# The written order of a graph layer's steps: a step's sums are turned back two shares and the queries' projection later, and a tile is joined behind that

## The chip, the core and the metric

The kernel runs on one core of a Trainium2 chip. The metric is the time of one launch on the device in microseconds, the median of seven runs. One further execution was taken with the hardware profiler; all durations below come from it.

## The reference, cut to what matters

Two layers work on 3125 nodes with 256 numbers each and on 100000 edges. A layer adds three things to its input: a graph attention over the edges, a token mixer, and then a feed-forward part. Only layer 0's graph attention and mixer bear on the change:

```
xn = layernorm(x)
x  = x + gnn(xn, edges) + mix(xn)           # layer 0; mix: 4 blocks of linear attention + GELU MLP
# gnn: two convolutions, each followed by batch norm and leaky relu
q, k, v = x @ wq, x @ wk, x @ wv            # 4 heads of 64
alpha   = sum(q[dst] * k[src], head) / 8
a       = softmax of alpha over the edges of one dst
out     = segment_sum(a * v[src], dst) + x @ ws
```

`gnn` and `mix` read the same input and do not need each other, so that the kernel can run them side by side.

## The kernel before, in words

Layer 0 puts the nodes in order of their number of edges and cuts them into 25 tiles of 128 nodes. Each tile has as many slots for edges as its largest node needs (64 in the first tile, 22 in the last, 833 in all). A tile's slots are worked off in two to four **steps** of one or two sub-steps with at most eight slots each; a convolution has 63 steps, the two convolutions 126. The rows of keys and values for one slot (512 numbers a node) are fetched by one indirect DMA that GpSimd issues (L707). Four buffers `kv` hold a sub-step each, so that the rows of step n+1 are fetched while step n is worked on; a buffer is free again when TensorE has read its values.

What a step does is written as letters, and the string `PATTERN` gives their order. Each letter issues instructions on the engines that it names, and TensorE, VectorE and ScalarE execute them exactly in that order, one engine by itself, waiting for each other by semaphores. GpSimd and SyncE are ordered by the scheduler. Read for step n:

- `K1`, `K0`: VectorE multiplies keys by queries and sums per head, for the second sub-step of n and the first of n+1 (L1074, L1077).
- `S`, `E`: VectorE takes bias and maximum (L1087 to L1091), ScalarE the exponential (L1101).
- `V0`, `V1`: VectorE sums the weights (L1108) and multiplies the values by them (L1114).
- `P0`, `P1b`: TensorE sums the values over the slots by transposing matmuls that accumulate (L200); `P1b` is that of step n-1's second sub-step. What comes out in PSUM is transposed.
- `Rb`, `Xb`, `Yb`: the sums of step n-1 are brought back. ScalarE copies them to SBUF (`accT`, L1133), TensorE turns them by two transposes into the other half of their PSUM tile (L214), ScalarE copies that to `res` (L1141).
- `M`, `N`: in a tile's last step, the maxima and sums of its steps are brought together (L1149 to L1167).
- `J`, `O`, `U`: in a tile's first step, the tile before is finished. `J` (VectorE, L1175) weighs the parts in `res` with each other, `O` (TensorE, L1555 and L1562) turns them and adds the skip projection, `U` adds the bias on ScalarE (L1570), takes the batch norm's statistics on VectorE (L1575) and stores.
- `T`, `B`: in the same step the next tile's nodes are turned (L1524) and brought to SBUF. `Q`: in a tile's second step its successor's queries are projected (L1538 and the bias at L129).
- `m`: one share of the mixer. The mixer is a list of small pieces, each with a part on TensorE and a `post` on ScalarE or VectorE that evicts it; five `m` stand in a step, and each takes as many pieces as are due. A piece's post is issued one piece after its TensorE part.

The mixer's lines in what follows: L189 projections, L1682 turned rows, L1751 keys, L1792, L1806, L1835 and L1960 attention, L1991 and L2009 the MLP with its bias at L129, L2017 and L1968 the additions to the result on VectorE.

The sums and the tile's output take their PSUM from one pool, `cps`, with two buffers; the queries from another with two; the mixer's pieces from a third with four. A step's sums keep their `cps` buffer from `P0` until `Yb` of the next step. Layer 1 has a pattern of its own, which is not touched.

These lines tie the letters to the functions:

```
P0=(True, lambda: self.sums(n, 0)),
P1b=(was["two"], lambda: self.sums(n - 1, 1)),
Rb=(n > 0, lambda: self.result(n - 1)),
Xb=(n > 0, lambda: self.turned(n - 1)),
Yb=(n > 0, lambda: self.kept(n - 1)),
J=(first and i > 0, lambda: self.join(i - 1)),
O=(first and i > 0, lambda: self.tiles[i - 1]["out"][0]()),
Q=(c == 1, lambda: self.q.__setitem__(i + 1, make())),
m=(True, lambda: mix(3 / PATTERN.count("m"))),
```

Of the kernel before, what the change touches and what calls it, by code (L numbers as in the profile page):

```python
# [1016 lines left out]
    sent.append(ins)  # L1017


PATTERN = "K1 m S E M P1b Rb m Xb Yb Q V0 J m P0 O V1 N m K0 T m U B".split()  # L1020


class SlotOrder:
# [156 lines left out]
    def run(self):  # L1180
# [18 lines left out]
        for n, t in enumerate(self.steps):  # L1199
# [8 lines left out]
            if more:  # L1208
# [25 lines left out]
                Q=(c == 1, lambda: self.q.__setitem__(i + 1, make())),  # L1234
                m=(True, lambda: mix(3 / PATTERN.count("m"))),
            )
            for what in PATTERN:
                if do[what][0]:
# [5 lines left out]
        for what, f in last.items():  # L1244
            if what in PATTERN and (what not in ("V1b", "P1b") or t["two"]):
                if what in ("Rb", "Xb", "Yb"):
                    f(n)
                else:
                    f(n, int(what[1]))
        if "Nb" in PATTERN:  # L1250
            self.join_sum(NQ - 1)
# [5 lines left out]
class EdgeOrder(SlotOrder):  # L1257


    HEADS, SCALE = 8, 1.0 / math.sqrt(32.0)  # L1260
    PATTERN = (
        "P1b D2 Rb D3 m K1 T0 Xb Yb S E M J m E0 Qt Qb m T1 D0 O m U Qm E1 Qk V0 m D1 T2 m "
        "V1 E2 m P0 T3 N m E3 K0 m"
    ).split()
# [86 lines left out]
    def run(self, ended):  # L1351
# [10 lines left out]
        self.keys(0, 0)  # L1362
        parts = self.PATTERN.count("m")
        for n, t in enumerate(self.steps):
# [2433 lines left out]
```

## Time and profile before

| | |
|---|---|
| median of 7 runs | 5315.23 us (5305.73 to 5320.78) |
| the profiled execution, its own time | 5315.53 us |
| its span in the profile | 5313.7 us |
| mean granted TensorE clock | 0.851 |
| busy: TensorE, VectorE, ScalarE, GpSimd | 4062, 3909, 1714, 3080 us |
| steps of convolution 1 | from 331 to 1490 us |
| steps of convolution 2 | from 1594 to 2787 us |

The profiled execution is 0.3 us above the median of the seven, so that sums made on it can be read as sums on the median. The change lies in the two stretches of steps, 2352 us together; everything else stays as it is. "Idle" of an engine is the time between the end of one of its instructions and the start of the next, and each idle stretch is put down to what ended last before it was over.

### The profile page before, as it was taken

To read this page: it belongs to the slowest core of one execution; us is meant where nothing else is said; L and a number is where in the kernel's file an instruction comes from. 1 tells how busy PE (TensorE), PEld (TensorE's weight loads), DVE (VectorE), ACT (ScalarE), POOL (GpSimd) and SP (SyncE) were. 2 spreads that over 40 slices of the span, in tenths; PEclk is the share of its full clock that TensorE was granted. 3 is DMA by queue.
4 is the path that set the end of the run, shared out by engine and by line. 5 is a ranking of instruction groups with operands and counts; after the bars stand their busy time and mean duration, and the time that the engine had idled before them with its cause. 6 is when DMAs were issued, how large, how long until landed. Compare 5 with 4: busy or idle time off the path is not lost. (4 is left out here: it accounts for less than half of the span.)

```text
span 5313.7 us, 54974 instructions
## 1 busy us (share of the span) xinstructions
PE 4062.2 (76%) x19016; PEld 2691.6 (51%) x19016; DVE 3909.2 (74%) x5861; ACT 1714.3 (32%) x3630; POOL 3080.3 (58%) x2945
## 2 busy tenths in 40 slices
PE   2557898768885688877885596987888887788778
PEld 1235675456644466555664463345455554444445
DVE  5268888878848888898873213469888888888957
ACT  1023334323342334443343111333333333333221
POOL 2466776657727577666753503257766767776720
PEclk8778999879997799988996797888788888888889
DMA  5166776667737577666765343545655655565610
GB/s 167 48 192 198 211 215 206 184 187 213 214 126 209 183 215 210 204 204 189 223 192 186 114 148 110 172 123 170 181 174 172 190 159 170 167 183 168 184 56 25
DMA packets 374305, 908.90 MB, mean 171 GB/s; under 512 B 94268, under 2 KB 170074, under 8 KB 373892
## 3 DMA queue, kind: packets, MB, share of 16 engines
q0 software_dynamic: 232624, 725.48, 46.3%
q1 hardware_dynamic: 134232, 165.02, 9.6%
q10 hardware_dynamic: 7162, 14.80, 0.7%
q8 instruction: 153, 2.51, 0.2%
q14 instruction: 134, 1.10, 0.1%
HBM read 813.62 MB, written 91.30 MB: 170 GB/s over the span
## 5 line engine op out<-in xcount | busy, mean ns | idle before, releaser
L707 POOL DMA_INDIRECT kv<-kvtab,slots x2499 | 2580.7, 1033 | 1144.0 <-issue 666.2
L1077 DVE TENSOR_REDUCE al<-kv 128x28 f32<-128x1792 f32 (+5 forms) x345 | 719.2, 2085 | 11.9
L200 PEld LDWEIGHTS cps<-ident,kv 128*128 128x128 f32 x4998 | 621.7, 152 | 145.7 <-issue 84.8
L200 PE MATMUL cps<-ident,kv 128*128 128x128 f32 x4998 | 670.7, 291 | 15.7 <-DVE kv L1114 10.4
L1316 DVE TENSOR_TENSOR kv<-kv,e 128x1024 f32<-128x1024 f32 x460 | 489.1, 1113 | 153.8 <-PE e L1305 63.4
L1074 DVE TENSOR_TENSOR kv<-kv,qa 128x1792 f32<-128x1792 f32 (+2 forms) x230 | 478.6, 2081 | 121.6 <-DMA kv<-kvtab,slots 100.6
L1114 DVE TENSOR_TENSOR kv<-kv,qa 128x1792 f32<-128x1792 f32 (+2 forms) x230 | 475.2, 2075 | 0.0
L1991 PE MATMUL mm<-hTm,w 128*128 128x500 f32 (+1 forms) x896 | 377.6, 563 | 28.8 <-DVE xcur L2017 23.6
L2009 PE MATMUL mm<-w,hid 128*125 128x256 f32 x1600 | 386.3, 391 | 11.0 <-ACT hid L1999 10.8
L2009 PEld LDWEIGHTS mm<-w,hid 128*125 128x125 f32 x1600 | 298.6, 195 | 63.5 <-ACT hid L1999 16.0
L1305 PE MATMUL e<-we,eaT 64*128 64x256 f32 x1666 | 290.3, 450 | 35.4 <-ACT eaT L1295 26.1
L1305 PEld LDWEIGHTS e<-we,eaT 64*128 64x128 f32 x1666 | 172.5, 210 | 181.2 <-ACT eaT L1295 60.4
L1991 PEld LDWEIGHTS mm<-hTm,w 128*128 128x128 f32 x896 | 160.4, 200 | 166.3 <-issue 126.1
L1074 DVE TENSOR_TENSOR kv<-kv,q 128x1792 f32<-128x1792 f32 (+2 forms) x115 | 239.3, 2081 | 1.4
L1114 DVE TENSOR_TENSOR kv<-kv,al 128x1792 f32<-128x1792 f32 (+2 forms) x115 | 239.2, 2080 | 0.0
L214 PE MATMUL cps<-ident,accT 128*128 128x128 f32 x378 | 88.2, 321 | 190.6 <-ACT accT L1133 190.4
L1682 PE MATMUL mm<-ident,xh 125*128 125x125 f32 x400 | 104.3, 358 | 168.7 <-ACT xh L1672 158.8
L707 POOL DMA_INDIRECT g<-ys,sloti x50 | 63.5, 1270 | 271.7 <-issue 235.4
L189 PE MATMUL mm<-wqv,hTm 128*125 128x512 f32 x400 | 193.8, 623 | 4.1 <-ACT kT L1763 4.1
L3159 PE MATMUL w<-sel,x 32*125 32x496 f32 x400 | 143.8, 681 | 44.1 <-ACT sq L3168 35.0
L214 PEld LDWEIGHTS cps<-ident,accT 128*128 128x128 f32 x378 | 50.5, 158 | 249.4 <-ACT accT L1133 236.0
L1999 ACT ACTIVATE hid<-mm,b 128x500 f32<-128x500 f32 (+1 forms) x224 | 134.5, 635 | 130.3 <-PE mm L1991 128.8
(421 smaller groups left out, 7245.1 us busy)
## 6 DMA issues: line engine op xcount, KB each, us to landing
kv<-kvtab,slots POOLq DMA_INDIRECT x2499, 3.7
w<-in_L_ffn_w_dram SPq DMA_DIRECT2D x32, 512.0 KB
qd<-qT SPq DMA_DIRECT2D x24, 500.0 KB
kvtab<-st SPq DMA_DIRECT2D x12, 1000.0 KB
qT<-qd SPq DMA_DIRECT2D x24, 500.0 KB
xTg<-xcols SPq DMA_DIRECT2D x24, 500.0 KB
w<-in_L_mix_W_dram SPq DMA_DIRECT2D x8, 1024.0 KB
xs<-zero SPq DMA_DIRECT2D x16, 512.0 KB
```

What stands on the lines that cost most here:

```text
L189: nc.tensor.matmul(ps, lhs(c), w(c), start=(c == 0), stop=(bias is None and c == n_chunks - 1))
L200: m = nc.tensor.matmul(ps[:, ch], src[:, ch], k.ident, start=(start and c == 0), stop=stop, is_transpose=True, skip_group_check=True,)
L214: k.nc.tensor.transpose(ps[:, ch], src[:, ch], k.ident)
L707: return k.nc.gpsimd.indirect_dma_start(out=out, out_offset=None, in_=table, in_offset=bass.IndirectOffsetOnAxis(ap=index, axis=0),)
L1074: nc.vector.tensor_tensor(kv[:, :m, :D], kv[:, :m, :D], q.unsqueeze(1).to_broadcast([128, m, D]), op=ALU.mult)
L1077: nc.vector.tensor_reduce(t["al"][:, b0 : b0 + m], self.heads(kv[:, :m, :D]), axis=AX.X, op=ALU.add)
L1114: nc.vector.tensor_tensor(v, v, t["w"][:, b0 : b0 + m].unsqueeze(3).to_broadcast([128, m, H, D // H]), op=ALU.mult)
L1305: self.k.nc.tensor.matmul(e[:, j % 2 * 2 + j // 2], eaT[r, j // 2], self.we[r], start=True, stop=True)
L1316: self.k.nc.vector.tensor_tensor(to, to, e[:, 2 * odd : 2 * odd + n].unsqueeze(2).to_broadcast([128, n, 2, D]), op=ALU.add,)
L1991: nc.tensor.matmul(ps[:, :w_], W["w1"][:, c, j * 128 : j * 128 + 128], o["hT"][:, c, :w_], start=(c == 0), stop=(c == 1),)
L2009: nc.tensor.matmul(ps[:P, :D], s["hid"][:, c, j * P : j * P + P], W["w2"][:, c, :], start=(c == 0), stop=False,)
L3159: nc.tensor.matmul(ps[:P, :496], o["x"][rows, tk], sel[rows], start=True, stop=True, tile_position=((h0 + b) * 32, 0),)
```

## The change

In `PATTERN` three groups of letters change places. Numbering the five `m` of a step 1 to 5: `Xb` and `Yb` stood after the second `m` and stand after the third; `Q` and `V0`, which followed them, now come before the third `m`; `J` follows `Yb` and `V0` as before, and with them stands behind the third `m` instead of ahead of it; `O` stood right after `P0` and now stands behind the fourth `m`. The number of instructions of each kind, the data, the buffers and the five shares are the same.

```diff
-PATTERN = "K1 m S E M P1b Rb m Xb Yb Q V0 J m P0 O V1 N m K0 T m U B".split()
+PATTERN = "K1 m S E M P1b Rb m Q V0 m Xb Yb J P0 V1 N m O K0 T m U B".split()
```

Engine by engine, with the shares as m1 to m5, the order of a step becomes:

```
TensorE before  m1 P1b m2 Xb Q m3 P0 O m4 T m5      after  m1 P1b m2 Q m3 Xb P0 m4 O T m5
VectorE before  K1 m1 S M m2 V0 J m3 V1 N m4 K0 m5 U   after  K1 m1 S M m2 V0 m3 J V1 N m4 K0 m5 U
ScalarE before  m1 E M Rb m2 Yb m3 m4 m5 U B        after  m1 E M Rb m2 m3 Yb m4 m5 U B
```

GpSimd's order of instructions is the same in both; on SyncE some loads and stores of the mixer and of the tiles change places by one.

## The prediction

> **What bounds the kernel now.** I read the page first. TensorE looks like the busiest engine, and one row there says that it idles 190.6 us ahead of the turning transposes.
>
> ```profile
> PE 4062.2 (76%) x19016; PEld 2691.6 (51%) x19016; DVE 3909.2 (74%) x5861; ACT 1714.3 (32%) x3630; POOL 3080.3 (58%) x2945
> ...
> L707 POOL DMA_INDIRECT kv<-kvtab,slots x2499 | 2580.7, 1033 | 1144.0 <-issue 666.2
> ...
> L214 PE MATMUL cps<-ident,accT 128*128 128x128 f32 x378 | 88.2, 321 | 190.6 <-ACT accT L1133 190.4
> ```
>
> A share over the span mixes stages, so the view by stretches comes next, for the steps of the two convolutions alone (columns: length, busy time of PE, PEld, DVE, ACT, POOL, granted clock, DMA share, GB/s).
>
> ```profile
> 331.00:1490.00 1159.00, 915.58 (x4424) 672.20 (x4425) 971.84 (x1404) 421.85 (x864) 772.44 (x816) 0.88 0.67 200
> 1594.00:2787.00 1193.00, 933.09 (x4473) 682.53 (x4473) 1003.92 (x1412) 443.45 (x924) 786.15 (x825) 0.87 0.68 203
> ```
>
> Here VectorE leads (84%), and GpSimd, whose 0.95 us instructions follow each other at 1.25 us (0.30 of it issue), is bound to 1627 x 1.25 = 2034 of 2352 us. TensorE's 79% count a clock of 0.88. So I asked the waits of VectorE, GpSimd and TensorE in 331 to 2787 us (columns: total us, times, longest).
>
> ```profile
> DVE den L1108 <- ACT qa L1101: 81.9, 63, 3.8
> DVE kv L1074 <- DMA kv<-kvtab,slots: 80.7, 49, 18.5
> DVE qm L1783 <- ACT vs L1781: 45.5, 27, 3.6
> DVE res L1175 <- ACT res L1141: 32.2, 18, 8.4
> DVE bst L1575 <- ACT o L1570: 19.3, 12, 2.4
> ...
> POOL kv L707 <- PE cps L200: 188.2, 48, 16.3
> ...
> PE cps L214 <- ACT accT L1133: 188.0, 63, 9.6
> ```
>
> VectorE waits for exponentials, gathers, mixer evictions and joins; TensorE's 188 us are what the change goes for. The timeline says what these 188 us hide. In a step where TensorE is early:
>
> ```profile
> 1184.99 0.37 ACT L1133 COPY accT<-cps 128x256 f32<-128x256 f32 x1
> 1185.23 2.28 DVE L1114 TENSOR_TENSOR kv<-kv,qa 128x2048 f32<-128x2048 f32 x1
> 1185.41 0.69 PE L214 MATMUL cps<-ident,accT 128*128 128x128 f32 x2 [5.95 <-ACT accT L1133]
> 1185.89 3.62 PE L2009 MATMUL mm<-w,hid 128*125 128x256 f32 x8
> 1189.52 2.41 PE L200 MATMUL cps<-ident,kv 128*128 128x128 f32 x16
> ```
>
> `Rb` stands in ScalarE's queue behind `E`, `E` waits for VectorE's softmax, and TensorE waits 5.95 us behind both with m3 ready. `P0` (L200) starts at 1189.52, though V0 ended at 1187.51. In a step where TensorE is late, nothing waits at L214, but the join does:
>
> ```profile
> 2689.40 2.01 DVE L1114 TENSOR_TENSOR kv<-kv,qa 128x1792 f32<-128x1792 f32 x1
> 2693.11 0.38 PE L214 MATMUL cps<-ident,accT 128*128 128x128 f32 x2
> 2693.33 1.89 PE L2009 MATMUL mm<-w,hid 128*125 128x256 f32 x8
> 2693.53 0.37 ACT L1141 COPY res<-cps 128x256 f32<-128x256 f32 x1 [2.63 <-PE cps L214]
> 2693.93 0.69 DVE L1175 TENSOR_TENSOR res<-res,qa 128x512 f32<-128x512 f32 x1 [2.52 <-ACT res L1141]
> ```
>
> VectorE stands 2.52 us, for `Yb`, which waits for `Xb`.
>
> **The change part by part.** Nothing is added or removed; each part moves work. I went through the 124 steps of the two stretches in the timeline that have a step before them.
>
> *Xb behind m3 and Q.* 63 steps show the stall. Q is five rows, some 1 us, and m3 takes 1.5 to 3.5 us; both now run inside it. What this gives `P0`, the next that others wait for, is less: it also needs V0, which ends 2.0 to 2.3 us after the exponential and had m3 beside it. For each step I put `Xb` at the later of "m3 done without the stall" and "Rb done", and `P0` at the later of `Xb` done and V0 done. In the step at 1185 `P0` gains 2.0 us. Summed, it starts 55 us earlier, 11 us of them given up again in second steps, where `P0` takes the `cps` buffer that `Yb`, now just ahead of it, has to free. So of 188 us some 130 turn into a wait for V0 at `P0`.
>
> *What `P0` earlier is worth.* GpSimd waits for a release at 57 places, 242 us (188.2 under L200, the rest under neighbours that end at the same time). Shortened by their step's gain these lose 38 us; but only where VectorE afterwards really waits for a gather does it reach the end, and there it is 17 us. In a third of the stalled steps the third share begins with a piece whose input (xh, ks) ScalarE brings only behind the exponential: 11 us. Bounds 0 and 38; I take 11, nearest to the steps that wait.
>
> *Evictions of m3 and m4 on VectorE.* By slot, VectorE waits 9 us for m3's pieces and 25 for m4's, nearly all in steps that join nothing. They come sooner by `P0`'s mean gain of 0.4 us and in stalled steps by the stall; I take 8 of these 34, bounds 0 and 15.
>
> *J behind m3.* This is on VectorE, which leads. J needs `Yb`, and that now follows m3, `Xb` (0.4 us) and m3's posts on ScalarE; VectorE reaches J 0 to 2.8 us after V0, as long as m3's posts take. In 22 of the 48 joining steps TensorE is late (no stall at L214), and there `Yb` moves by the whole share: at 2689 by 1.7 us, the wait from 2.5 to 4.2. Summed over the 48 the wait is 48 us where it was 17 (the other 15 of the 32.2 are the two joins behind the last step, which stay): +31. In 7 us of these a gather wait follows in the same step and swallows it: +24. Queued behind J on VectorE are V1, N, K0; `P1b` waits for V1, but starts 5 to 10 us behind it, so nobody but VectorE itself pays. Bounds 5 (the gain of `P0` carried into the late steps) and 31.
>
> *O behind m4, Q ahead of V0.* `O` ends 3.6 us after J by the median, its eviction's statistics (L1575) start at 6.6, and a share of m4 is 1.89 us: in most tiles it still fits. In nine tiles `O` ended at 4.9 us or later, and the excess is just under 1 us: +8, bounds 0 and 17 (a whole share each). Behind it on ScalarE stand `B` and the next step's `E`, which waits for VectorE anyway; the store it issues on SyncE's queue has no reader before the convolution's end. Q earlier costs nothing: its input was brought in the step before. GpSimd's queue is not reordered.
>
> Sum: 24 + 8 - 11 - 8 = +13, from 5315.5 to about 5328.
>
> **Two rules.** After the stall at 1185 eight L2009 take 3.62 us, and 1.89 at 2693: the clock stood at half rate. The Trainium skill, TensorE: Matmul & The Clock Gate, section "HAM oscillation — how this bites in real kernels", says that a TensorE idle for more than about 3.4 us falls to half its clock. Twenty stalls are longer; as an estimate by that page each costs a window of half rate, 1.7 us, 34 in all, and by it the sum would be 5294 if all of this reached the end. Against the change speaks Perfetto Trace Analysis, section "Identifying the Most-Contended Engine": improve the engine with the highest occupancy, here VectorE with 84%; by it TensorE's gain is worth nothing, and 5315.5 + 32 = 5347 is left.
>
> **The rivals.** *Nothing to see.* The gains are near their upper ends in half of the places, +24 + 8 against 17 + 15: 5315.5, give or take 10. For it speaks that both sides are small sums of stalls of 1 to 2 us with slack around them; against it, that losses lie on VectorE and gains on an engine that waits.
>
> *Faster: TensorE's stall was the path.* One mechanism: `P0` releases the gather buffer, GpSimd starts earlier, K0 and K1 find their rows. GpSimd waits for L200 48 times, and 80.7 us of VectorE's waits are for gathers. If the whole 38 us arrive and 15 of evictions, with J at 24: 5315.5 - 38 - 15 + 24 = 5286. It decides once the 57 waits are followed by a gather that is used at once; in most of the places the gathered rows lie 5 to 20 us before K reads them, which speaks against it.
>
> *Slower by all that J and O can cost:* J unabsorbed 31, O 17, no gain: 5315.5 + 48 = 5364.
>
> **How the numbers follow.** About 0.2%, 10.6 us, is what can be told from no change. Slower by more than that (the sum, up to the full cost) gets 0.44, within it 0.30, faster 0.26. The prediction is the sum, 5328. The range runs from the faster rival's 5286 to the full cost, 5364, which leaves out the tails of both; slower alone is 5326 to 5364.
>
> **What would show it.** Right: TensorE's wait at L214 for L1133 falls from 188 us below 90, and L200 begins to wait for L1114 (8 us in the steps before) by about 100; VectorE's wait at L1175 rises from 32 to 55 or more; bst at L1575 from 19 to about 27; GpSimd's wait for L200 falls by 10 to 40. Wrong: VectorE's waits at L1175 stay at 32 (then late steps have become early ones), or those for gathers fall by more than 30 us, and the two stretches together, 2352 us, get shorter.

## The result and the profile after

The changed kernel takes 5335.93 us (median of 17 runs) where the kernel before takes 5313.33 us (41 runs beside them): a ratio of 1.0039, 95% interval 1.0029 to 1.005. It is slower by some 21 us, more than can be told from no change, and inside the range; the forecast of 5328 us had the sign and the mechanism, and 60% of the size.

The profiled execution after has a span of 5336.7 us, 23.0 more than before, at the same mean clock of 0.851. The timeline says where they are. From the softmax of its second step to the end of its last join, convolution 1 took 1165.0 us and takes 1175.0, convolution 2 took 1146.7 and takes 1157.5: together +20.8. Another 2.8 us come ahead of the first of these softmaxes, and the rest of the kernel takes what it took. So the 20.8 us are what has to be explained.

The page first. The row of the turning transposes (L214) is gone from its list of costliest groups, with the 190.6 us that TensorE idled there; the idle time stands in other rows now.

```profile
PE 4068.3 (76%) x19016; PEld 2712.2 (51%) x19016; DVE 3908.8 (73%) x5861; ACT 1712.2 (32%) x3630; POOL 3082.1 (58%) x2945
...
L200 PE MATMUL cps<-ident,kv 128*128 128x128 f32 x4998 | 699.1, 299 | 77.2 <-DVE kv L1114 51.1
...
L1682 PE MATMUL mm<-ident,xh 125*128 125x125 f32 x400 | 108.6, 364 | 217.3 <-ACT xh L1672 207.2
```

The view by stretches, over the same two windows as before (length, busy time of PE, PEld, DVE, ACT, POOL, granted clock, DMA share, GB/s):

```profile
331.00:1490.00 1159.00, 905.89 (x4362) 669.66 (x4361) 965.19 (x1390) 417.09 (x856) 778.06 (x818) 0.88 0.67 200
1594.00:2787.00 1193.00, 920.21 (x4385) 680.73 (x4384) 991.21 (x1384) 434.12 (x905) 792.62 (x833) 0.86 0.68 202
```

VectorE gets through less in the same time (1956 us of work instead of 1976), at nearly the same clock and DMA rate. TensorE does too (1826 us instead of 1849): its idle time as a whole did not fall. What holds it is in the waits (total us, times, longest), taken from 331 to 2815 us:

```profile
DVE den L1108 <- ACT qa L1101: 81.9, 63, 3.8
DVE res L1175 <- ACT res L1141: 80.1, 37, 7.4
DVE kv L1074 <- DMA kv<-kvtab,slots: 61.2, 41, 18.5
DVE qm L1783 <- ACT vs L1781: 46.8, 27, 3.6
DVE bst L1575 <- ACT o L1570: 20.5, 16, 2.4
...
POOL kv L707 <- PE cps L200: 187.2, 48, 18.2
...
PE cps L214 <- ACT accT L1133: 49.2, 17, 6.6
PE cps L200 <- DVE kv L1114: 47.9, 32, 3.6
```

TensorE's wait at L214 fell from 188.0 to 49.2 us, and that paid little by itself, as the experiments show. VectorE's books close: its wait for the join's input (L1175) rose by 47.9 us, its waits for gathered rows fell by 19.5 and those put down to "issue" ahead of L1074 from 10.9 to 5.1, and the others that changed (L1783 +1.3, L1575 +1.2, L1968 -1.5, L2017 -2.7) nearly cancel. That makes +21, for the 20.8 us that the two convolutions got longer.

The two steps that the prediction followed, after. First the counterpart of the one at 1185, where TensorE was early (timeline):

```profile
1199.42 2.28 DVE L1114 TENSOR_TENSOR kv<-kv,qa 128x2048 f32<-128x2048 f32 x1
1199.60 0.56 PE L214 MATMUL cps<-ident,accT 128*128 128x128 f32 x2 [4.20 <-ACT accT L1133]
1201.80 3.65 PE L200 MATMUL cps<-ident,kv 128*128 128x128 f32 x16 [1.64 <-issue]
1201.95 0.68 DVE L1175 TENSOR_TENSOR res<-res,qa 128x512 f32<-128x512 f32 x1
```

`P0` starts 0.1 us after V0 instead of 2.0, as worked out, and the join does not wait. Then the counterpart of the one at 2689, where TensorE was late:

```profile
2714.01 0.37 ACT L1133 COPY accT<-cps 128x256 f32<-128x256 f32 x1 [0.61 <-PE cps L200]
2714.54 4.00 PE L2009 MATMUL mm<-w,hid 128*125 128x256 f32 x16
...
2718.90 0.37 ACT L1141 COPY res<-cps 128x256 f32<-128x256 f32 x1 [3.19 <-PE cps L214]
2719.31 0.69 DVE L1175 TENSOR_TENSOR res<-res,qa 128x512 f32<-128x512 f32 x1 [3.74 <-ACT res L1141]
```

The sums were in SBUF at 2714.38, but their two transposes (2718.49) and `Yb` come behind 16 matmuls of the mixer, the second and the third share, and VectorE stands 3.74 us where it stood 2.52. Two more steps show what else can lie between. In the one at 882 the transposes are done at 877.46, before V0 begins:

```profile
877.08 0.38 PE L214 MATMUL cps<-ident,accT 128*128 128x128 f32 x2
...
877.64 2.01 DVE L1114 TENSOR_TENSOR kv<-kv,qa 128x1792 f32<-128x1792 f32 x1
...
879.77 0.16 DVE L1667 SCALAR_TENSOR_TENSOR ln_nm<-ln_mv,ln_rs 125x4 f32<-125x4 f32 x1
879.97 2.08 ACT L1672 ACTIVATE xh<-xcur,ln_nm,ln_rs 125x256 f32<-125x256 f32 x4 [3.80 <-DVE ln_nm L1667]
...
881.95 0.35 ACT L1141 COPY res<-cps 128x256 f32<-128x256 f32 x1
882.34 0.95 DVE L1175 TENSOR_TENSOR res<-res,qa 128x768 f32<-128x768 f32 x1 [2.40 <-ACT res L1141]
```

`Yb` (L1141) now stands in ScalarE's queue behind the third share's post. That post takes 2.08 us, and it waits for a small mixer operation of VectorE (L1667) which stands behind V0 there. So VectorE waits in `J` for ScalarE, which had waited for VectorE: 2.40 us where the same join did not wait before. And in the step at 1859 the share itself was not ready:

```profile
1859.36 3.75 PE L1960 MATMUL mm<-cw,qT 128*125 128x256 f32 x8 [2.49 <-DMA qT<-qd]
1862.90 0.63 PE L214 MATMUL cps<-ident,accT 128*128 128x128 f32 x2
...
1863.97 0.95 DVE L1175 TENSOR_TENSOR res<-res,qa 128x768 f32<-128x768 f32 x1 [6.20 <-ACT res L1141]
```

TensorE waited 2.49 us for a load, then ran eight matmuls in 3.75 us, and everything behind them in its queue waited too, `Xb` included: 6.20 us on VectorE, where this join stood 1.60 before.

### The profile page after: what moved, and what is told of

It is laid out like the page before. It is cut to its first block, busy times and chain, and to the rows that moved or that the text cites. A ratio compares the mean times of both kernels' runs of the same rounds, so it can differ in the third digit from the quotient of the medians.

```text
span 5336.7 us, 54998 instructions
## 1 busy us (share of the span) xinstructions
PE 4068.3 (76%) x19016; PEld 2712.2 (51%) x19016; DVE 3908.8 (73%) x5861; ACT 1712.2 (32%) x3630; POOL 3082.1 (58%) x2945
## 2 busy tenths in 40 slices
DMA packets 374305, 908.90 MB, mean 170 GB/s; under 512 B 94268, under 2 KB 170074, under 8 KB 373892
## 5 line engine op out<-in xcount | busy, mean ns | idle before, releaser
L200 PE MATMUL cps<-ident,kv 128*128 128x128 f32 x4998 | 699.1, 299 | 77.2 <-DVE kv L1114 51.1
L200 PEld LDWEIGHTS cps<-ident,kv 128*128 128x128 f32 x4998 | 642.5, 157 | 177.8 <-issue 78.4
L1316 DVE TENSOR_TENSOR kv<-kv,e 128x1024 f32<-128x1024 f32 x460 | 489.2, 1113 | 146.7 <-PE e L1305 70.6
L1074 DVE TENSOR_TENSOR kv<-kv,qa 128x1792 f32<-128x1792 f32 (+2 forms) x230 | 478.5, 2081 | 99.7 <-DMA kv<-kvtab,slots 82.6
L1114 DVE TENSOR_TENSOR kv<-kv,qa 128x1792 f32<-128x1792 f32 (+2 forms) x230 | 475.3, 2075 | 0.0
L2009 PE MATMUL mm<-w,hid 128*125 128x256 f32 x1600 | 385.0, 390 | 23.0 <-ACT hid L1999 22.6
L2009 PEld LDWEIGHTS mm<-w,hid 128*125 128x125 f32 x1600 | 298.3, 194 | 76.8 <-ACT hid L1999 28.6
L1682 PE MATMUL mm<-ident,xh 125*128 125x125 f32 x400 | 108.6, 364 | 217.3 <-ACT xh L1672 207.2
L1074 DVE TENSOR_TENSOR kv<-kv,q 128x1792 f32<-128x1792 f32 (+2 forms) x115 | 239.3, 2081 | 1.4
L1114 DVE TENSOR_TENSOR kv<-kv,al 128x1792 f32<-128x1792 f32 (+2 forms) x115 | 239.2, 2080 | 0.0
L1682 PEld LDWEIGHTS mm<-ident,xh 125*128 125x128 f32 x400 | 62.4, 174 | 269.0 <-ACT xh L1672 262.1
L2325 DVE TENSOR_TENSOR ye<-o,b 128x256 f32<-128x256 f32 x64 | 27.2, 425 | 197.6 <-PE o L2321 197.6
L3168 ACT ACTIVATE sq<-w,r 125x496 f32<-125x496 f32 x200 | 125.0, 671 | 140.7 <-PE w L3159 140.3
```

Source lines behind the costliest of these rows:

```text
L200: m = nc.tensor.matmul(ps[:, ch], src[:, ch], k.ident, start=(start and c == 0), stop=stop, is_transpose=True, skip_group_check=True,)
L1074: nc.vector.tensor_tensor(kv[:, :m, :D], kv[:, :m, :D], q.unsqueeze(1).to_broadcast([128, m, D]), op=ALU.mult)
L1114: nc.vector.tensor_tensor(v, v, t["w"][:, b0 : b0 + m].unsqueeze(3).to_broadcast([128, m, H, D // H]), op=ALU.mult)
L1316: self.k.nc.vector.tensor_tensor(to, to, e[:, 2 * odd : 2 * odd + n].unsqueeze(2).to_broadcast([128, n, 2, D]), op=ALU.add,)
L1682: nc.tensor.transpose(ps[:, j * P : j * P + P], o["xh"][:, j, c * 128 : c * 128 + 128], k.ident[:P, :P],)
L2009: nc.tensor.matmul(ps[:P, :D], s["hid"][:, c, j * P : j * P + P], W["w2"][:, c, :], start=(c == 0), stop=False,)
```

## The experiments

The theory after this comparison: the loss is VectorE's wait in `J` for the later `Yb`, and so it lies in the steps that join a tile alone. The first rival: the later `Xb` and `Yb` cost something in every step. The second: `O` behind the fourth share costs it. The first four kernels were timed on one chip, where the kernel before took 5321.24 us.

**New order only where no tile is joined.** The loop takes the old order in a tile's first step.

```diff
+FIRST = "K1 m S E M P1b Rb m Xb Yb Q V0 J m P0 O V1 N m K0 T m U B".split()
-            for what in PATTERN:
+            for what in FIRST if first else PATTERN:
```

> The new order in the steps that join no tile, the old order in a tile's first step. Theory (the join on VectorE waits for a later Yb, and that is the whole loss): the wait at L1175 is back at 30 to 36 us, and the time is at or below the kernel before, ratio 0.996 to 1.000 (5292 to 5313 us). Rival A (the late Xb itself costs: P0 waits for the PSUM buffer and for V0, in every step): three fifths of the loss stay, since 76 of the 124 steps are late, 1.002 to 1.003. Rival B (the output behind m4): the output is back at its place, so 0.999 to 1.001.

Measured: 5311.52 us, ratio 0.9987 [0.9976, 0.9999]. Its waits:

```profile
DVE kv L1074 <- DMA kv<-kvtab,slots: 78.7, 49, 18.4
DVE res L1175 <- ACT res L1141: 31.8, 18, 9.0
```

With the join back at its place the loss is gone, and the join's wait is the old one to 0.4 us, while TensorE's wait at L214 is 98.4 us instead of 188.0. That the later transposes cost in every step, 1.002 or more, is refuted.

**New order only where a tile is joined.** The same edit with the two orders exchanged.

> The reverse: the new order only in a tile's first step, the old order in all others. Theory (join): the wait at L1175 is 75 us or more and the ratio 1.004 to 1.007 (5334 to 5351 us), the whole loss and none of the small gain of the other steps. Rival A (late Xb in every step): 1.001 to 1.002. Rival B (the output behind m4): 1.003 to 1.005 with the wait at L1575 above 25 us.

Measured: 5349.51 us, ratio 1.005 [1.0032, 1.0069], with 70.6 us at L1175 (a little under the 75 expected) and 69.6 us for gathers. All of the loss is here; the two halves, -0.0013 and +0.005, make 0.0037, close to the 0.0039 of the whole change. The ratio alone would also fit the rival of the output, but that one asked for more than 25 us at L1575, where 17.8 stand.

**New order, the join behind V1.** This keeps everything of the change but `J`'s place.

```diff
-... Xb Yb J P0 V1 N m O ...
+... Xb Yb P0 V1 J N m O ...
```

> The new order, but J stands behind P0 and V1, so that VectorE has 1.8 to 2.3 us of its own work between V0 and J while Yb comes. Theory (join): the wait at L1175 falls from 80 to 25 to 40 us, of which 15 are the two last joins, and the ratio to 0.997 to 1.001 (5297 to 5319 us). Rival A (late Xb in every step) and rival B (the output behind m4): both are still there, 1.003 to 1.005, and VectorE's waits at L1175 only move to other lines.

Measured: 5318.01 us, ratio 0.999 [0.9978, 1.0003]. V1, which has no need of the turned sums, covers the wait:

```profile
DVE kv L1074 <- DMA kv<-kvtab,slots: 82.6, 56, 18.6
DVE res L1175 <- ACT res L1141: 29.7, 15, 8.8
```

Against the changed kernel only `J` moved, and 50.4 us of join waits went while 21.4 us of gather waits came back: 29 us by the waits, 26 by the ratios (0.0049 of 5315, with an interval of some 9 us to either side). This is the price of `J` waiting.

**New order, the output right behind P0.**

```diff
-... J P0 V1 N m O K0 ...
+... J P0 O V1 N m K0 ...
```

> The new order with O put back right behind P0; J stays behind m3. Theory (join): 1.002 to 1.004 (5324 to 5334 us), the wait at L1175 stays at 70 to 85 us; TensorE now also waits for J in O, a few us at L1555. Rival A: 1.003 to 1.005. Rival B (the output behind m4 is the loss): 0.999 to 1.001, with L1575's wait below 20 us.

Measured: 5342.34 us, ratio 1.0046 [1.003, 1.0062], 78.2 us at L1175. Putting `O` back returns nothing that can be told, so the second rival falls. The ratio is above the 1.002 to 1.004 expected, which its interval includes; TensorE's waits for `J` in `O` came as 7.5 us at L1555.

**The parts of the change alone.** Four more kernels were tried in a session on another chip, in which the unchanged kernel itself took 5713.39 us, and its ratios have intervals of 0.2 to 0.27% to either side, which settle nothing of this size. They were: `J` alone behind the third share; `O` alone behind the fourth; the old order with `J` behind V1 and `O` behind the fourth share; and the new order in the other steps with that third order in the joining ones.

> The old order with J alone moved behind m3; Xb and Yb stay ahead of m3 and Q, O stays behind P0. Theory (not J's place costs, but that Yb comes late for it): the wait at L1175 falls to 20 to 30 us, of which 15 are the two last joins, and the ratio is 0.998 to 1.001 (5302 to 5319 us). Rival C (J behind m3 is itself the loss, since V1 and K0 queue behind it and m3's evictions wait for TensorE): 1.002 to 1.005.

> The old order with O alone moved behind m4. Theory (join): 0.999 to 1.001; the wait at L1575 rises from 19 to at most 25 us, and the forecast's 8 us for this part were too much. Rival B (the output behind m4): 1.002 or more with L1575 above 30 us.

> The old order with J behind P0 and V1 and O behind m4, Xb and Yb early. If a late Yb is all that VectorE ever waits for at J, the wait at L1175 falls from 32 to the 15 to 20 us of the two last joins and the ratio is 0.996 to 0.999 (5292 to 5308 us). If the joins' waits had been hidden by the gathers anyway, 0.999 to 1.001, with the waits at L1074 higher by what L1175 lost.

> The new order in the steps that join no tile; in a tile's first step Xb and Yb stay ahead of m3, J stands behind P0 and V1, O behind m4. Theory: the gain of the late Xb in the other steps (0.9987 when tried alone) and the join's remaining wait add up: 0.995 to 0.998 (5287 to 5302 us), L1175 at 15 to 22 us. If the two gains are the same one (VectorE waits for the gathers instead): 0.998 to 0.9995.

Measured, in this order: 0.9991 [0.9964, 1.0017], 1.0019 [0.9994, 1.0044], 1.0013 [0.9992, 1.0033], 1.0007 [0.9979, 1.0034]. All include no change. The waits that were expected can't be read there either: in all four kernels, whether `O` moved or not, 50 to 86 us stand at L1575 behind L1570 and another 34 to 53 that the profile puts down to "issue". Three of them were therefore run again, with the first experiment beside them, on a third chip, where the kernel before took 5321.93 us.

`J` alone behind the third share:

```diff
-... Rb m Xb Yb Q V0 J m P0 O V1 ...
+... Rb m Xb Yb Q V0 m J P0 O V1 ...
```

> Only J moves: it goes behind m3, with Xb, Yb, V0, Q and O at their old places. Theory (the loss is the wait for the later Yb, not J's later place): Yb is long done, VectorE's wait at L1175 stays at or below the 32 us of the kernel before, and the ratio is 0.997 to 1.001. Rival (J's later place itself, with V1 and K0 behind it, is the loss): 1.002 to 1.004.

Measured: 0.999 [0.9975, 1.0004], 24.5 us at L1175. `J` a share later costs nothing as long as `Yb` is early: it is how late `Yb` comes for `J` that costs, not `J`'s own place.

`O` alone behind the fourth share:

```diff
-... m P0 O V1 N m K0 ...
+... m P0 V1 N m O K0 ...
```

> Only O moves: it goes behind m4, everything else at its old place. My forecast had a price of 8 us for this, 0 to 17: a ratio of 1.0015, and VectorE's wait at L1575 up from 19 to about 27 us. The run without this part of the change showed nothing of it: by that the ratio is 0.999 to 1.001 and the wait stays within 3 us.

Measured: 0.9996 [0.9986, 1.0006]. The time is as expected. The wait is not: it came nearly as large as the forecast of 27 us, while this run was expected to stay within 3 us of 19:

```profile
DVE bst L1575 <- ACT o L1570: 25.5, 20, 2.4
```

L1575 went from 19.3 to 25.5 us, and the time did not follow: by the interval the move costs between -7 and +3 us, which leaves out the 8 of the forecast. Why the wait does not reach the end was not tried; it stands near the end of a step.

New order where nothing is joined, `J` behind V1 with early transposes where a tile is joined:

```diff
+FIRST = "K1 m S E M P1b Rb m Xb Yb Q V0 m P0 V1 J N m O K0 T m U B".split()
```

> New order in the steps that join no tile; in a tile's first step Xb and Yb stand at their old place and J behind V1, with O behind m4. If the later transposes gain a little where nothing joins, and J gains a little where it need not wait, the two add up: 0.997 to 0.999, L1175 below 32 us. If they are the same gain twice, or none: 0.999 to 1.001.

Measured: 5314.05 us, 0.9987 [0.9976, 0.9999]. L1175 is down to 16.1 us in three waits, so that hardly any of the 48 joins waits any more, and L1575 is up to 31.9. As far as the intervals tell, the gains do not add up: this is what the first experiment had without touching the joining steps. Of the join's 18 us of waiting in the kernel before, 12.6 stand at L1575 instead.

The first experiment again:

> New order only in the steps that join no tile, beside the kernel that also moves J. If the earlier 0.9987 was a gain of the later transposes: 0.998 to 0.9995 again. If it was chance: 0.9995 to 1.001. A loss of 1.002 or more would speak against the theory that the loss lies in the joining steps.

Measured: 5312.23 us, 0.9988 [0.9976, 1.0001], 31.9 us at L1175. Twice the same: a tenth of a per cent under the kernel before, at the edge of what can be told. It is the fastest version of those run, together with the one above it, and worth some 6 or 7 us, with an interval from 0 to 13; the two kernels at 0.999 can't be told from it.

## Why the prediction was right, and where its sum was off

*Xb behind m3.* It held. L214's wait is 49.2 us, below the 90 named. The gain of `P0` held too: its start behind the end of V0, summed over the 124 steps, fell from 275 to 217 us, 58 us where 55 were worked out, or 44 without the 11 us that second steps were to give up again. What did not come is the size of the wait for V0 at `P0`: L200 waits 47.9 us for L1114, not some 100. Even with the 19.1 us in eleven waits of `P0` that the profile puts down to "issue", each of which ends 0.1 us behind V0 like the one at 1201.80, it is 67. Another 48 us stand at the mixer's turned rows, where L1682's wait for L1672 rose from 109.9 to 158.3: the share now ahead of `Xb` waits for inputs that ScalarE brings behind the exponential, which the prediction saw in a third of the stalled steps.

*J behind m3.* This term carried the result, and both of its halves were too small. The wait over the 48 joins rose from 17.9 to 66.3 us, +48 where +31 was forecast, the upper bound of this term. In the 22 steps that showed no stall at L214 before, where the prediction put the growth, the wait rose from 13.6 to 39.0 us. The miss lies in the other 26, for which the prediction names no growth: from 4.3 to 27.2. The assumption that failed there is that `Yb` follows m3 at once and early enough. In seven of them, 17 us of the 27, TensorE was no longer early, and the transposes ended 0.9 to 3.0 us behind V0. In ten, 10 us, the transposes were done before V0's end and `Yb` stood behind the mixer's posts on ScalarE, as at 882; the prediction had named these posts and given them no price of their own. On the other side gathers swallowed about 20 us of the wait, not 7. The net of both, 26 us by the ratios with and without it, is close to the 24 of the sum; that is luck, since the wait and what swallows it were both too small, by 17 and 13 us.

*P0 earlier, evictions, O.* -11, -8 and +8 made -11 together. The kernel with all of them and without the waiting join has a ratio of 0.999, -5 us with an interval from -12 to +2. `O` is 0 of it, by two runs (1.0046 with it put back beside 1.0039, and 0.9996 for it alone). Its wait was sized well where it was alone (25.5 against 27), and was wrongly put on the path; in the changed kernel it hardly came (20.5). So of the 19 us of gains some 5 came. These two errors partly cancelled, and with 2 us more for `J` they are the 8 us between 13 and the 21 measured.

*GpSimd's wait for L200* was to fall by 10 to 40 us, and stayed (188.2 to 187.2); with its neighbours L1792 and L1682 it rose from 221.0 to 246.5. It was a bad witness. GpSimd's work is fixed, so its idle time grows with the stretch, here by 20.8 us, whatever becomes of single releases; in the kernel with the join behind V1, whose two convolutions are 8.6 us shorter than in the kernel before, the same three lines make 213.2.

*The two rules.* By the Trainium skill, TensorE: Matmul & The Clock Gate, section "HAM oscillation — how this bites in real kernels", the 20 long stalls were worth an estimated 34 us of half rate. (The section's own example counts 1.67 us throttled a stall and half of that as lost, which would make an estimated 17 us here.) The price of one stall is in the rows of this case: after the stall at 1185 the eight L2009 take 3.62 us at a granted clock of 0.50, at 2693 they take 1.89 at 1.00. The saving did not come: with the stalls at L214 down from 188 to 49 us the granted clock of the two stretches is 0.88 and 0.86, hardly other than before (0.88 and 0.87). The half rate moved instead: after the 4.20 us stall at 1199 the 16 matmuls of `P0` take 3.65 us at a clock of 0.50, where the same 16 took 2.41 at 0.79 in the step at 1185. And other long stalls took the place of those that went: from 331 to 2787 us TensorE idles longer than 3.4 us in 54 places before and in 52 after, at all lines together. The rule of the Trainium skill, Perfetto Trace Analysis, section "Identifying the Most-Contended Engine", to improve the engine with the highest occupancy, was the better guide, though the 5347 drawn from it went past the mark: 139 us off TensorE's largest wait, much of which came back at other lines, were worth some 5, and 29 us net more on VectorE cost 26.

*The rivals.* "Slower by all" named the right place with too high a price; "TensorE's stall was the path" would have needed gather waits to decide, and these fell by 19.5 us only because the join waited in their stead. When `J` was moved out of the way they were back at 82.6.

## What to carry to other kernels

When a short transfer step is moved behind a filler on a shared in-order queue, look for its consumer on the busiest engine and move that consumer by the same amount, behind work that does not need it; here that was one letter, and it made the difference between +0.39% and -0.1%, the latter within noise. Price the delay by the filler with its own waits and its evictions on the other queue that the step crosses, not by its matmuls alone. And before a long wait is counted as a gain, find where the bottleneck engine stops: of 139 us taken off TensorE's largest wait hardly any reached the end.

## What the runs showed of the hardware

The same unchanged kernel took 5321 and 5322 us on two chips and 5713 us on another, at a granted clock of 0.83 instead of 0.85. On that one, with `J` alone moved, the two convolutions took 1302 and 1290 us, where the same kernel took 1168 and 1143 on one of the two. With the longer time waits appear that the profile puts down to no releaser: 33.9 us of "issue" ahead of VectorE's L1575, none in the list of the same kernel on the faster chip. The bytes are the same (908.90 MB), so the DMA rate of 159 GB/s over the whole span instead of 171 only says again that the span is longer. Why, no run here tells; the ratios of that session, with intervals of up to 0.27% to either side, are too coarse for this question.
